# Slots of 4128 bytes instead of 4096, and 39 of them instead of 40

## The chip, the cores and the metric

The kernel runs on one core of a Trainium2 chip. Time is the device time of one execution in microseconds (us); of several runs the median is given. Beside the time of a run stands its span: from the first to the last instruction of the program that the profiler recorded.

A core has TensorE (PE in the profile, its weight loads PEld), VectorE (DVE), ScalarE (ACT), GpSimd (POOL) and SyncE (SP), each with its own queue of instructions that it takes in order. DMAs are issued from the queues of SP and POOL and move data by 16 DMA engines. The engines wait for each other by semaphores. The on-chip memory has 128 partitions; an address below is a byte within a partition.

## The reference

All in float32. With `xn` the normalised input (8192 tokens of 512 numbers),

```
out = x + attention(xn) + moe(xn)

attention: feats   = 1/sqrt(512) * exp(xis) * exp(xn @ (xis*proj).T - 0.5*|xn|^2 * xis^2)
           weights = the same of input_weights
           out     = feats @ weights.T                                   (512 x 512)

moe:       scores = sigmoid(xn @ router_w)                               (64 experts)
           4 of 8 groups of experts by their best score, of these the 8 best experts
           weights of the 8: scores / their sum * 2.5
           each expert takes its first 256 tokens:
             (silu(t @ gate_w[e]) * (t @ up_w[e])) @ down_w[e]           (512 -> 256 -> 512)
           out = weighted sum over the experts + a shared expert of the same form
```

## The kernel before

**Products.** Each float32 operand is split in two (`upper` on ScalarE writes the high part as float32r, `rest` on VectorE the low part), and `products` makes three passes of matmuls: high by high, high by low, low by high. So a weight tile that a DMA brings is first split into two further tiles, and only these are read by TensorE.

**Stages.** The token blocks of 512 (16 of them) go through `look_up` (turned by TensorE, routed, their rows written to `xnw` in HBM) and, every second one, through `dense` (shared expert and attention); this takes the first 400 us or so. Then comes the loop over the 64 experts (`for i in range(E + 1)`), with the attention of the other blocks (`late_attention`) put between its steps. At its end `ends` does the shared expert of the remaining blocks, from about 1146 us on.

**An expert.** At step `i` of the loop SyncE is given the loads of the gate and up weights of expert `i + 2` (`load_gates`, L744, two tiles) and the down weights of expert `i + 1` (`load_down`, L749, one tile). TensorE does `hidden(i)`: 48 matmuls for gate and up, and the 8 transposes of the rows of expert `i + 1` (`turn_slots`, L773), which `gather` (L756) has brought. Then ScalarE and VectorE split the gates of expert `i + 1` (`split_gates`), TensorE does `down(i - 1)` (12 matmuls), and POOL adds its rows to the output by an indirect DMA (L831). Then the down weights of expert `i` are split (`split_down`).

**The slots.** Nearly all large tiles stand in one pool, `four`, with one tag: `kib4` hands out a slot of it. A tile of 128 partitions by 1024 float32 numbers fills 4096 bytes of each partition. Which slot a tile gets and what it waits for is settled when the program is built: the first instruction that writes a tile (a DMA for loads, an engine for others) waits for the last reader of the tile that had the slot before. All slots of a pool's tag have the size of the largest tile asked for under the tag.

In the loop over the experts, an expert takes 12 slots: 2 for gate and up, 4 for their splits, 1 for down, 2 for its splits, 2 for the turned rows `gT`, 1 for `ehT`. The line search (`at`) takes one more for each four experts, and the seven blocks of `late_attention` take 10 each (4 `xT`, 4 `fU`, 2 `yb`), spread over the 64 experts. Eleven slots are held through the whole loop: `fW` 4, `pT` 4, `ye` 3.

In the built program the first slot begins at byte 25504 of a partition, and the others follow each other at once. The pools `rows` (gathered rows), `rt` (small tiles) and `act` (work tiles of 2048 bytes) follow behind the slots; `const` stands ahead of them.

Of the kernel before, what the change touches and what calls it, by code (L numbers as in the profile page):

```python
# [11 lines left out]
I32 = mybir.dt.int32  # L12
# [6 lines left out]
P = 128  # L19
# [3 lines left out]
E = 64  # L23
# [12 lines left out]
RC = R // P  # L36
IC = I // P
NH = CAP // P
SLOTS4 = 40
UT = TB // 2  # L40
GAP = 5
NCH = T // P
# [11 lines left out]
def rfs_attention_moe_kernel(  # L54
# [23 lines left out]

    four = ctx.enter_context(tc.tile_pool(name="four", bufs=SLOTS4))
    rows = ctx.enter_context(tc.tile_pool(name="rows", bufs=4))  # L80
# [3 lines left out]
    def kib4(shape, name, dt=FPR):  # L84
        return four.tile(shape, dt, tag="four", name=name)
# [131 lines left out]
    nc.gpsimd.iota(slot_i, pattern=[[P, NH]], base=0, channel_multiplier=1)  # L217
    slot = const.tile([P, NH], FP, name="slot")
    nc.gpsimd.tensor_copy(slot, slot_i)
    erow_i = kib4([P, E], "erow_i", I32)  # L220
    nc.gpsimd.iota(erow_i, pattern=[[1, E]], base=-E, channel_multiplier=0)
    erow = const.tile([P, E], FP, name="erow")
    nc.gpsimd.tensor_copy(erow, erow_i)
# [782 lines left out]
```

## Time and profile before

| | |
|---|---|
| three runs | 1308.88, 1309.06, 1309.46 us; median 1309.06 |
| the profiled execution | 1309.75 us, span 1308.0 us |
| granted TensorE clock | 0.999 |
| PE busy | 1295.1 us of the span (99%), 7648 matmuls |
| DVE, ACT, POOL busy | 925.9 (71%), 644.1 (49%), 587.0 (45%) us |
| DMA | 338.61 MB, mean 259 GB/s |

The page gives busy time by engine, the same over 40 slices of the span, the DMA queues, the chain of work that ended last, and groups of equal instructions with the mean of one, the idle time of the engine ahead of them and what ended it. Three more views of the trace are used: the waits (who waited for whom, in total, how often, the longest), the stages (busy time of each engine between two times), and the timeline (instructions in the order of time). SPq is the queue of SyncE, which issues DMAs; a wait of SPq is time in which its next DMA could not be issued yet.

### The profile page before, as it was taken

What the parts mean: (1) busy time and instruction counts of PE and PEld (TensorE: products, weight loads), DVE (VectorE), ACT (ScalarE), POOL (GpSimd) and SP (SyncE); (2) the same over time, 40 slices, a digit from 0 to 9 for tenths busy, and PEclk for the clock granted to TensorE, in tenths of its full rate; (3) what the DMA queues carried; (4) which work ended last, traced back from release to release, by engine and by line L of the source; (5) the groups of instructions that cost most, each with busy time, mean ns of one, the idle gap of its engine ahead of it and who ended that gap; (6) DMA issues with size and microseconds to landing.
All of it is one profiled execution on the core that took longest, in us unless ns stands there. A gap on an engine that the chain in (4) does not pass through costs nothing.

```text
span 1308.0 us, 21401 instructions
## 1 busy us (share of the span) xinstructions
PE 1295.1 (99%) x7648; PEld 1136.1 (87%) x7648; DVE 925.9 (71%) x1922; ACT 644.1 (49%) x1017; POOL 587.0 (45%) x692
## 2 busy tenths in 40 slices
PE   8999999999999999999999999999999999999998
PEld 6888888888888988999999999999999999988886
DVE  7978768867765776678677677777776776643555
ACT  5643544454432555566566465656665565540111
POOL 3122022123106766777677767767766654210000
PEclk9999999999999999999999999999999999999999
DMA  7655675675586989999999999999999999784995
GB/s 255 242 209 207 242 282 200 240 286 212 198 306 191 308 236 322 263 288 274 303 288 251 282 290 270 264 302 290 275 257 297 286 260 238 204 240 167 319 319 193
DMA packets 189498, 338.61 MB, mean 259 GB/s; under 512 B 15952, under 2 KB 87632, under 8 KB 189392
## 3 DMA queue, kind: packets, MB, share of 16 engines
q1 hardware_dynamic: 153456, 245.93, 54.4%
q0 software_dynamic: 35936, 91.32, 29.8%
q8 instruction: 60, 0.98, 0.3%
q14 instruction: 46, 0.38, 0.1%
HBM read 220.66 MB, written 104.99 MB: 249 GB/s over the span
## 4 chain that ended last, share of the span: by engine, by line
PE 87%; DVE 7%; DMA 3%; SPq 1%; issue 1%; ACT 1%; POOL 0%; ACTq 0%; DVEq 0%
PE ps_gu L108 41%; PE ps_e L108 13%; PE ps_o L108 12%; PE ps_fu L108 6%; PE ps_y L108 5%; PE ps_t L773 3%; PE ps_f L108 3%; PE ps_x L333 2%; PE ps_l L366 1%; DMA xb<-in_L_attn_x_dram 1%; DVE st L277 1%; DVE f L495 1%; SPq L264 1%; DVE xT_l L101 1%; DVE fT L101 1%
## 5 line engine op out<-in xcount | busy, mean ns | idle before, releaser
L831 POOL DMA_INDIRECT out_dram<-ye,who x128 | 232.7, 1818 | 181.5 <-ACT ye L830 120.8
L108 PE MATMUL ps_gu<-gT,gu_h 128*128 128x256 f32 x2048 | 292.5, 285 | 0.0
L108 PEld LDWEIGHTS ps_gu<-gT,gu_h 128*128 128x128 f32 x2048 | 265.4, 190 | 8.9 <-ACT gu_h L98 4.7
L703 POOL DMA_INDIRECT at<-upto,line x128 | 131.9, 1030 | 76.0 <-DVE first_of L697 37.3
L101 DVE TENSOR_TENSOR gu_l<-gu,gu_h 128x1024 fp32r<-128x1024 f32 x128 | 155.0, 1221 | 14.3 <-ACT gu_h L98 13.4
L108 PE MATMUL ps_gu<-gT,gu_l 128*128 128x256 f32 x1024 | 164.9, 283 | 0.0
L756 POOL DMA_INDIRECT xg<-xnw,who x128 | 141.7, 1107 | 40.0 <-issue 30.0
L108 PE MATMUL ps_e<-d_h,ehT 128*128 128x512 f32 x512 | 147.8, 390 | 0.0
L108 PEld LDWEIGHTS ps_gu<-gT,gu_l 128*128 128x128 f32 x1024 | 142.6, 191 | 3.4 <-DVE gu_l L101 0.7
L98 ACT CAST gu_h<-gu 128x1024 fp32r<-128x1024 f32 x128 | 132.1, 1047 | 0.0
L830 ACT ACTIVATE ye<-ps_e,we 128x512 f32<-128x512 f32 x128 | 87.6, 687 | 84.5 <-PE ps_e L108 84.2
L108 PEld LDWEIGHTS ps_e<-d_h,ehT 128*128 128x128 f32 x512 | 94.7, 188 | 18.8 <-ACT d_h L98 0.2
L98 ACT CAST ehT<-sg 128x512 fp32r<-128x512 f32 x64 | 39.9, 623 | 123.1 <-DVE sg L503 112.0
L248 POOL TENSOR_TENSOR a<-rstd,ve 128x4 f32<-128x4 f32 x45 | 10.2, 227 | 200.5 <-DVE rstd L244 198.0
L503 DVE SCALAR_TENSOR_TENSOR sg<-sg,ps_gu 128x512 f32<-128x512 f32 x64 | 43.9, 686 | 72.1 <-PE ps_gu L108 72.0
L101 DVE TENSOR_TENSOR gT<-ps_t,gT 128x512 fp32r<-128x512 f32 x128 | 82.0, 682 | 17.1 <-ACT gT L98 17.1
L101 DVE TENSOR_TENSOR d_l<-d,d_h 128x1024 fp32r<-128x1024 f32 x64 | 78.2, 1221 | 11.7 <-ACT d_h L98 11.6
L509 ACT ACTIVATE f<-f,ab 128x512 f32<-128x512 f32 x64 | 46.3, 723 | 73.1 <-DVE f L495 72.4
L108 PE MATMUL ps_o<-fW_h,fT 128*128 128x512 f32 x288 | 79.8, 391 | 0.2 <-ACT fT L98 0.2
L108 PE MATMUL ps_e<-d_l,ehT 128*128 128x512 f32 x256 | 79.2, 390 | 0.0
L108 PE MATMUL ps_o<-d_h,hT 128*128 128x512 f32 x256 | 79.1, 396 | 0.0
L501 ACT ACTIVATE sg<-ps_gu 128x512 f32<-128x512 f32 x64 | 38.2, 597 | 77.7 <-PE ps_gu L108 77.7
(181 smaller groups left out, 2520.0 us busy)
## 6 DMA issues: line engine op xcount, KB each, us to landing
gu<-in_L_ffn_gate_w_dram SPq DMA_DIRECT2D x64, 512.0 KB
gu<-in_L_ffn_up_w_dram SPq DMA_DIRECT2D x64, 512.0 KB
d<-in_L_ffn_down_w_dram SPq DMA_DIRECT2D x64, 512.0 KB
xnw<-xw SPq DMA_DIRECT2D x32, 577.0 KB
xb<-in_L_attn_x_dram SPq DMA_DIRECT2D x32, 512.0 KB
out_dram<-xb SPq DMA_DIRECT2D x32, 512.0 KB
xT_h<-turned SPq DMA_DIRECT2D x30, 512.0 KB
xT_l<-turned SPq DMA_DIRECT2D x30, 512.0 KB
```

Of the source, the lines that this page charges most:

```text
L98: return nc.scalar.copy(dst, src)
L101: return on.tensor_tensor(dst, src, hi.bitcast(FP), ALU.subtract)
L108: last["pe"] = nc.tensor.matmul(ps, w[c][a], v[c][b], start=(start and part == 0 and c == 0), stop=(stop and part == 2 and c == n - 1),)
L333: last["turn"] = nc.tensor.transpose(pr[:, ts(s, P)], src(s)[:, ts(kc, P)], ident if dt is FP else ident_r)
L501: nc.scalar.activation(dst, g, AF.Tanh, scale=0.5)
L503: nc.vector.scalar_tensor_tensor(dst, dst, 0.5, u, ALU.mult, ALU.mult)
L509: nc.scalar.activation(f, f, AF.Exp, scale=ab[:, rc : rc + 1])
L703: nc.gpsimd.indirect_dma_start(out=at[:, e % TE, h, :], out_offset=None, in_=upto, in_offset=bass.IndirectOffsetOnAxis(ap=line[:, e, h : h ...
L756: nc.gpsimd.indirect_dma_start(out=xgs[e][:, h, :], out_offset=None, in_=xnw, in_offset=bass.IndirectOffsetOnAxis(ap=who[:, e, h : h + 1], ...
L773: turned_s = nc.tensor.transpose(pr[:, c, ts(h, P)], xr[:, h, ts(c2 * 2 + c, P)], ident_r)
L830: nc.scalar.activation(ye[:, h, :], po, AF.Copy, scale=wes[e][:, h : h + 1])
L831: now = nc.gpsimd.indirect_dma_start(out=out, out_offset=bass.IndirectOffsetOnAxis(ap=who[:, e, h : h + 1], axis=0), in_=ye[:, h, :], in_o ...
```

## The change

```diff
-SLOTS4 = 40
+SLOTS4 = 39
...
-    erow_i = kib4([P, E], "erow_i", I32)
+    erow_i = kib4([P, 1032], "erow_i", I32)[:, 0:E]
```

`erow_i` is a small tile of the beginning, used once. Asked for with 1032 numbers it makes 4128 bytes the size of every slot of the pool; of it, the same 64 columns are used as before. 40 slots of 4096 bytes are 163,840 bytes of a partition; 39 slots of 4128 are 160,992. Every tile that filled a slot leaves the last 32 bytes of it unused.

In the built program every engine has the same instructions in the same order. What differs: the slot that a tile stands in, and so its address and what its first writer waits for; the slots begin at 25504, 29632, 33760, ... instead of 25504, 29600, 33696, ...; and `rows`, `rt` and `act` begin 2848 bytes lower.

## The prediction

> **What bounds the kernel now.** I read first the busy time by engine, then the stages, then the waits of TensorE, and last the waits of SyncE's queue, because the change touches a kernel's supply of tiles.
>
> ```profile
> PE 1295.1 (99%) x7648; PEld 1136.1 (87%) x7648; DVE 925.9 (71%) x1922; ACT 644.1 (49%) x1017; POOL 587.0 (45%) x692
> ...
> PE   8999999999999999999999999999999999999998
> DMA  7655675675586989999999999999999999784995
> ```
>
> TensorE has work for 1295.1 of 1308.0 us; the other engines have a quarter of their time or more to spare. DMA is at nine tenths from about 430 us on, so loads deserve a look. Busy PE is a model, so the waits must say the same. Those of PE and PEld:
>
> ```profile
> PE ps_x L333 <- DMA wi<-_attn_input_weights_dram: 4.8, 2, 3.6
> PE ps_bu L447 <- DVE prior_r L437: 1.0, 4, 0.3
> ...
> PEld ps_gu L108 <- ACT gu_h L98: 4.9, 16, 0.4
> PEld ps_x L333 <- POOL padded L256: 3.5, 1, 3.5
> ```
>
> The numbers are the total, the count and the longest. Apart from the start (`wi` must land) nothing holds TensorE for more than fractions of a microsecond. The stage 600 to 700 us, all inside the loop over the experts, as columns PE, PEld, DVE, ACT, POOL, granted clock, DMA share, GB/s:
>
> ```profile
> 600.00:700.00 100.00, 100.00 (x683) 92.20 (x682) 74.48 (x114) 58.34 (x84) 71.28 (x55) 1.00 1.00 287
> ```
>
> TensorE sets the time there, at full clock. Now the queue that the slots do hold back, in the window of the expert loop (430 to 1140 us):
>
> ```profile
> SPq L744 <- PE ps_gu L108: 191.8, 37, 10.0
> SPq L744 <- DVE gu_l L101: 88.5, 24, 6.6
> ...
> SPq L744 <- PE ps_e L108: 59.5, 23, 8.1
> ```
>
> L744 issues the gate and up loads. SyncE stands 340 us in these three rows alone, waiting for the last reader of the tile that had the slot before. So the slots do limit how early a load starts; whether that matters depends on when the load is needed.
>
> **The change part by part.**
>
> *One slot fewer.* An expert takes 12 slots; `at` adds 16/64 = 0.25 and `late_attention` 7 × 10/64 = 1.1, together 13.3. An expert lasts as long as TensorE takes for it: 68 matmuls and transposes of its own and 7 × 96/64 = 10.5 of the late attention, 78.5, at 683 in 100 us: 11.5 us. So a slot is handed out every 11.5/13.3 = 0.86 us. Eleven slots are held through the loop; of the other 29 one goes. A tile is then given a slot that is freed one hand-out later: on average 0.86 us later. Slots are freed in bursts, so single loads move by nothing or by several us; the longest single wait of SPq above, 10.0 us, is the upper bound that I take, nothing the lower. The value is 0.86 us, since it follows from counts.
>
> Against this stands how early the loads are. The timeline of SPq and ACT around 805 to 845 us:
>
> ```profile
> 805.21 1.50 SPq L744 DMA_DIRECT2D gu<-in_L_ffn_up_w_dram  x1
> 806.82 0.45 SPq L749 DMA_DIRECT2D d<-in_L_ffn_down_w_dram  x1
> ```
>
> ```profile
> 827.65 2.00 ACT L98 CAST gu_h<-gu 128x1024 fp32r<-128x1024 f32 x2
> ...
> 835.75 1.05 ACT L98 CAST d_h<-d 128x1024 fp32r<-128x1024 f32 x1
> ```
>
> The tile issued at 805.21 is split as the second of the two at 827.65, some 23 us later; the down tile issued at 806.82 is split at 835.75, 29 us later (another down tile, issued an expert before, stands between them). The landing of a load is the last update of its semaphore. Over the 128 gate and up loads it comes 7.7 us (median; longest 15.9) after the issue, and the split follows at least 8.4 us later (median 16); over the 64 down loads 10.2 us (longest 18.1), at least 7.1 us left. So a mean delay of 0.86 us is taken from a reserve of at least 7.1 us: **0 us**. The cover is that reserve; if it is gone, ScalarE waits at the split for the load, and behind it the `gT` of the next expert and the scaling of `ye`, which TensorE and POOL wait for. That ACT does not wait for such loads now can be seen in its group, whose idle time has no DMA as its end:
>
> ```profile
> L98 ACT CAST gu_h<-gu 128x1024 fp32r<-128x1024 f32 x128 | 132.1, 1047 | 0.0
> ```
>
> A rule of the Trainium skill speaks against the change here: its page Perfetto Trace Analysis, section Optimization Strategy, says that a gap repeating on the engine that should be saturated can mean too little room for the next tile, by the number of buffers. If TensorE had such gaps and each expert gained one hand-out, the sum would be 64 × 0.86 = 55 us, 1364 us. The rows show no such gap (PE 100.00 of 100.00), so I count 0.
>
> Other tiles that take slots: `xT` of the last stage is the tightest. Its low half is used 1.0 to 3 us after landing (from 1209 us on). But SPq there stands in L163 for the result that it stores (91.7 us in total for `xo`), not in L576 for a slot, so its loads do not move. The `xb` loads of the first stage have nothing in reserve in places (the chain has 1% of the span, 13 us, in their DMA); SPq waits for slots at L151 by 1.5 us in four cases, so I allow 0 to 4 × 0.86 = 3.4 us there and take 0: in that stage slots are freed by work long past. Engines that write a slot themselves (`gT`, `ehT`, `fU`, the splits) get one freed some 28 hand-outs before, 24 us; 0.
>
> *Addresses.* The DMAs first. No row before tells apart two starts, since all slots of the program before begin at 160 past a multiple of 256 (25504 and steps of 4096). The skill's page DMA: Bandwidth & Descriptors, section How a descriptor splits into AXI transactions, says that a transaction begins at a multiple of 256 bytes and that the bytes ahead of an unaligned start cost beats of 32 bytes. By it each piece now costs 5 beats too many; with steps of 4128 the starts spread over all eight multiples of 32, a mean of 3.5. A gate piece of 1024 bytes goes from 37 to 35.5 beats (-4%), a piece of 2048 bytes from 69 to 67.5 (-2%). If landing followed beats, a gate load would land 0.3 us earlier (an estimate: 4% of 7.7), which nothing waits for; the 13 us of `xb` in the chain would shrink by 2%, 0.3 us. By the rows, where loads mostly wait for each other, it is 0. I take 0 and keep -0.3; and +0.3 the other way, since the rule is not shown here for writes.
>
> The engines. Operations of one shape cost the same in and out of the slots:
>
> ```profile
> L101 DVE TENSOR_TENSOR gT<-ps_t,gT 128x512 fp32r<-128x512 f32 x128 | 82.0, 682 | 17.1 <-ACT gT L98 17.1
> L101 DVE TENSOR_TENSOR ehT<-sg,ehT 128x512 fp32r<-128x512 f32 x64 | 44.0, 688 | 26.1 <-ACT ehT L98 26.1
> ...
> L108 PEld LDWEIGHTS ps_f<-xT_h,pT_l 128*128 128x128 f32 x144 | 27.0, 188 | 5.6
> L366 PEld LDWEIGHTS ps_l<-xT_l,rwp 128*128 128x128 f32 x64 | 12.0, 188 | 2.7
> ```
>
> `sg` stands in `act`, `rwp` in `const`, not 4096 bytes apart from anything. If distances of a multiple of 4096 cost something, the slots' rows would be longer. 0 us.
>
> *Sum.* Span 1308.0 + 0 (slots) + 0 (addresses) = 1308.0; the profiled execution took 1309.75, that is 1.75 around the span, and was 0.7 above the median of the runs, 1309.06. Predicted: **1309.0 us**, the median unchanged.
>
> **The rivals.**
>
> *Slower by loads that come late.* The mechanism is the first edit with the upper bound: bursts make a freed slot late by up to 10 us instead of 0.86. It decides from about 7 us on, the smallest reserve. At 10 us, four places in the loop run short (loads issued around 429, 795, 865 and 877 us, with reserves of 8.8, 7.1, 8.4 and 8.4 us), by 1.2 + 2.9 + 1.6 + 1.6 = 7.3 us: 1316 us. For it: SPq's long waits. Against it: the mean is an eighth of the bound.
>
> *Engines that read or write at another speed.* One nanosecond on each of 7648 matmuls is 7.6 us, so 1301 or 1317 us. For it: TensorE is the bound, and nothing hides it. Against it: the equal rows above, which cover the weight loads, not the moving operand.
>
> *Faster by DMAs.* The -0.3 us above, at most some 2 us if all `xb` loads gain a tenth: 1307 to 1308.7, within 0.2%.
>
> *That nothing changes because the size is not taken up* is excluded: the built program has the slots 4128 bytes apart.
>
> **How the numbers follow.** 0.2% is 2.6 us, about what a measurement of this kernel can tell from no change. All hidden (with the DMA gain in it): 0.80. Late loads: 0.10, slower. Engines slower 0.04, engines faster 0.06. So faster 0.06, same 0.80, slower 0.14. The likeliest case reaches from 1307 (DMA gain) to 1311 (half of the 3.4 us at `xb`); the range takes that and the smaller late loads (one place of 2.9 us added to 1309.5): 1307.0 to 1312.5.
>
> **What would show it.** Right: PE and PEld waits as before; in the loop, as in the trace before, 227 ns from the start of a matmul of 512 columns to the next (median) and 120 of 256; SPq's waits at L744 some tens of us longer; no wait of ACT `gu_h` or `d_h` for a DMA. Wrong by slots: rows `ACT gu_h L98 <- DMA gu` or `ACT d_h L98 <- DMA d`, with PE idle after them. Wrong by addresses: another mean for the same shape of a matmul, cast or subtraction, or other times to landing.

## The result

| | before | after |
|---|---|---|
| median of four runs | 1309.26 us (1308.88 to 1310.26) | 1315.80 us (1315.13 to 1316.76) |
| span of the profiled execution | 1308.0 us | 1314.3 us |

The ratio is 1.005, 95% interval 1.0037 to 1.0062: the change makes the kernel slower by half a per cent, outside the predicted range of 1307.0 to 1312.5 us.

The page of the kernel after, busy time by engine and the slices of PE and DMA:

```profile
PE 1301.7 (99%) x7648; PEld 1131.3 (86%) x7648; DVE 927.0 (71%) x1922; ACT 644.0 (49%) x1017; POOL 586.5 (45%) x692
...
PE   8999999999999999999999999999999999999998
...
DMA  7655675675586989999999999999999999784995
```

TensorE has the same 7648 matmuls and 6.6 us more to do; the other engines differ from before by 1.1 us at most. Did it wait? The waits of PE and PEld after:

```profile
PE ps_x L333 <- DMA wi<-_attn_input_weights_dram: 6.0, 3, 3.6
PE ps_lt L383 <- ACT lt L376: 0.8, 2, 0.7
```

```profile
PEld ps_gu L108 <- ACT gu_h L98: 3.6, 12, 0.4
PEld ps_x L333 <- POOL padded L256: 3.6, 1, 3.6
```

No new wait of more than 1 us, and less waiting for `gu_h` than before (4.9 us). Nor does ScalarE wait for the load of an expert's weights; its group of casts still has no idle time ahead of it:

```profile
L98 ACT CAST gu_h<-gu 128x1024 fp32r<-128x1024 f32 x128 | 132.0, 1046 | 0.0
```

So the time is in the matmuls themselves. The chain of work in the order of time, from 1160 us on, where TensorE does little but matmuls of 512 columns; columns are start, length, what, how many matmuls. Before:

```profile
1160.13 10.88 PE ps_f L108 x48
1171.01 5.44 PE ps_gu L108 x24
1176.45 12.24 PE ps_o L108 x54
1188.69 5.44 PE ps_gu L108 x24
```

After:

```profile
1163.61 11.16 PE ps_f L108 x48
1174.77 5.57 PE ps_gu L108 x24
1180.34 12.54 PE ps_o L108 x54
1192.88 5.57 PE ps_gu L108 x24
```

24 matmuls took 5.44 us and now take 5.57: 227 and 232 ns each, and so within 0.03 us in every group of 24 of this stage. In the loop over the experts the groups of 24 matmuls of 256 columns behind those of 512 went the other way. Before (the same view, at 717 us):

```profile
717.40 2.87 PE ps_gu L108 x24
```

After (at 609 us):

```profile
609.44 2.83 PE ps_gu L108 x24
```

Over the whole trace I took the time from the start of each matmul to the start of the next, between matmuls of one width, without the first interval of each stretch of such matmuls and without the longer gaps (over 253 ns for 512 columns, over 147 ns for 256). This mean is called the pace below. It went from 227.7 to 232.1 ns for 512 columns and from 119.7 to 118.1 ns for 256.

That is the whole difference. Added up over pairs of equal matmuls in the two traces: 3547 intervals that begin with a matmul of 512 columns give +14.6 us, 2999 with one of 256 columns -4.5 us, longer gaps became 3.1 us shorter (2.1 us of it in the first 410 us, as if stalls that are waited for anyway took up some of the slower pace), and the rest gives -0.7: +6.3 us, as the spans say (1314.3 - 1308.0). By stage it is +3.5 us up to 414 us, -0.5 in the loop over the experts, where both widths meet, and +3.3 from 1139 us on.

### The profile page after: what moved, and what is told of

Read it like the earlier page. It is cut to its first block, busy times and chain, and to the rows that moved or that the text cites. A ratio compares the mean times of both kernels' runs of the same rounds, so it can differ in the third digit from the quotient of the medians.

```text
span 1314.3 us, 21375 instructions
## 1 busy us (share of the span) xinstructions
PE 1301.7 (99%) x7648; PEld 1131.3 (86%) x7648; DVE 927.0 (71%) x1922; ACT 644.0 (49%) x1017; POOL 586.5 (45%) x692
## 4 chain that ended last, share of the span: by engine, by line
PE 96%; DVE 2%; ACT 0%; DMA 0%; issue 0%; POOL 0%; SPq 0%; DVEq 0%; ACTq 0%
PE ps_gu L108 41%; PE ps_o L108 14%; PE ps_e L108 14%; PE ps_f L108 8%; PE ps_y L108 6%; PE ps_fu L108 6%; PE ps_t L773 3%; PE ps_l L366 2%; PE ps_x L333 2%; PE ps_lt L383 1%; PE ps_bu L458 0%; DMA wi<-_attn_input_weights_dram 0%; DVE st L277 0%; DVE xo L549 0%; DVE pT_l L101 0%
## 5 line engine op out<-in xcount | busy, mean ns | idle before, releaser
L108 PE MATMUL ps_gu<-gT,gu_h 128*128 128x256 f32 x2048 | 289.3, 283 | 0.0
L756 POOL DMA_INDIRECT xg<-xnw,who x128 | 138.3, 1080 | 40.1 <-issue 29.6
```

The lines of the kernel that those rows point to most:

```text
L108: last["pe"] = nc.tensor.matmul(ps, w[c][a], v[c][b], start=(start and part == 0 and c == 0), stop=(stop and part == 2 and c == n - 1),)
L756: nc.gpsimd.indirect_dma_start(out=xgs[e][:, h, :], out_offset=None, in_=xnw, in_offset=bass.IndirectOffsetOnAxis(ap=who[:, e, h : h + 1], ...
```

## The experiments

The first theory after the result: what changed for TensorE is only where its operands stand. Slots of 4096 bytes put moving operand and weights at a *distance* (start of the moving operand less start of the weights) that is a multiple of 4096 plus multiples of 512 inside the tiles; slots of 4128 give distances of 0, 32, ... 224 past a multiple of 256. Theory A: the pace depends on that distance. Theory B: the missing slot. Theory C: the start of an operand by itself.

The next four kernels ran on one chip, on which the kernel before took 1331.57 us (median, at a granted clock of 0.990 to 0.997 instead of 0.999); every ratio below is to the kernel before on the same chip.

**Count alone.**

```diff
-SLOTS4 = 40
+SLOTS4 = 39
```

> Only the count: 39 slots of 4096 bytes. Theory A (the pace of TensorE's matmuls depends on how far apart, within 256 bytes, the moving operand and the weights start; all distances here are multiples of 4096 plus offsets inside the tiles that are multiples of 512): 1309 us as before, 227 ns from start to start of matmuls of 512 columns and 120 ns of 256 columns. Theory B (the missing slot delays loads): 1316 us as with the whole change.

Measured: 1330.39 us, ratio 0.9986 (0.9971 to 1.0001); pace 227.7 and 119.6 ns. Theory B falls.

**Distance alone.**

```diff
-    erow_i = kib4([P, E], "erow_i", I32)
+    erow_i = kib4([P, 1032], "erow_i", I32)[:, 0:E]
```

> Only the distance: 40 slots of 4128 bytes. Theory A: 1316 us (1315 to 1317), 232 ns for 512 columns and 118 ns for 256 columns as with the whole change. Theory B: 1309 us.

Measured: 1338.37 us, ratio 1.0057 (1.0039 to 1.0074), 6.8 us more; pace 232.1 and 118.0 ns. The whole effect is in this line. (`rows`, `rt` and `act` move by 1280 bytes here, a multiple of 256, so their place within 256 bytes is not the cause.)

**Start of all slots, 32 bytes on.**

```diff
+    const.tile([P, 8], FP, name="spare")
     four = ctx.enter_context(tc.tile_pool(name="four", bufs=SLOTS4))
```

> 40 slots of 4096 bytes, but the first begins 32 bytes later, at 192 past a multiple of 256 instead of 160. Theory A (only the distance between two operands counts): 1309 us, 227 and 120 ns. Theory C (the start of an operand itself counts, by its place within 64 or 256 bytes; after the change half of the starts are multiples of 64, none was before, and here all are): 1316 us or farther from 1309, with another pace of the matmuls.

Measured: 1332.21 us, ratio 1.0009 (0.9996 to 1.0022); pace 227.7 and 119.6 ns. In the built program all slots now begin at multiples of 64. Theory C falls for this shift; with it agrees that in the trace after, the pace of 512 columns is 231.8 to 232.4 ns for every one of the eight starts of the moving operand within 256 bytes (by the addresses of the built program), and 231.6 to 232.3 for those of the weights.

**38 slots, 4352 bytes apart.**

```diff
-SLOTS4 = 40
+SLOTS4 = 38
-    erow_i = kib4([P, E], "erow_i", I32)
+    erow_i = kib4([P, 1088], "erow_i", I32)[:, 0:E]
```

> 38 slots of 4352 bytes (17 times 256), so that distances are multiples of 256 and seldom of 4096. Theory A with a period of 256 bytes: 1309 us, 227 and 120 ns. Theory A with a longer period (512 to 4096 bytes): 1313 us or more, pace as with 4128. Theory B: slower than 1316 us, since two slots are missing.

Measured: 1331.20 us, ratio 0.9992 (0.9977 to 1.0007); pace 227.7 and 119.6 ns. A distance need only be a multiple of 256, and two slots fewer cost nothing that can be measured either. The same pieces of the chain with 40 slots of 4128 bytes:

```profile
1184.60 11.17 PE ps_f L108 x48
1195.77 5.58 PE ps_gu L108 x24
1201.34 12.55 PE ps_o L108 x54
```

and with 38 of 4352:

```profile
1181.79 10.88 PE ps_f L108 x48
1192.67 5.44 PE ps_gu L108 x24
1198.11 12.24 PE ps_o L108 x54
```

**39 slots, 4224 bytes apart**, another chip (before: 1328.73 us):

```diff
-SLOTS4 = 40
+SLOTS4 = 39
-    erow_i = kib4([P, E], "erow_i", I32)
+    erow_i = kib4([P, 1056], "erow_i", I32)[:, 0:E]
```

> 39 slots of 4224 bytes (4096 + 128): distances are 0 or 128 past a multiple of 256. Theory A with a period of 256 bytes: between the two, 512 columns at 229 to 232 ns, 256 columns at 118 to 120 ns, a ratio to the kernel before of 1.002 to 1.005. A period of 128 bytes would give the pace and the time of before (ratio 1.000).

Measured: 1337.66 us, ratio 1.0059 (1.0039 to 1.0079); pace 231.2 and 118.9 ns. So 128 bytes is not a period. The paces lie where expected; the ratio is above the upper end that I gave, since I had counted on half of the matmuls keeping 227 ns, and only few did. Why is seen under "What runs before".

**The matmuls alone.** The body of the kernel is replaced by this (cut at `...`), so nothing of the model is computed; `weights` and `moving` are two tiles in float32r. It was run once.

```
for cols in (512, 256):
    for order in (range(8), range(7, -1, -1)):
        for shift in order:
            ps = ps_mm.tile([P, cols], FP, tag="mm", name=f"by_{words[shift]}")
            for n in range(64):
                at = n % 4 * P + shift * 8
                nc.tensor.matmul(ps, weights[:, ts(n % 8, P)], moving[:, at : at + cols], ...)
```

> Matmuls alone, nothing of the model: one weight tile and one moving tile, 64 matmuls for each of eight distances between them (0, 32, ... 224 bytes past a multiple of 256), for 512 and for 256 columns, once with growing and once with falling distance; no other engine works meanwhile, and all outputs but the last are thrown away, the last stands for the whole output. Theory A: from start to start at distance 0: 227 ns for 512 columns and 120 ns for 256 columns; at the other distances 230 to 234 ns for 512 columns, and for 256 columns 113 to 118 ns at 192 and no uniform value at the others. Theory D (the pace comes from what other engines or DMAs do at the same addresses): the same pace at all eight distances.

The timeline of PE, `by_six` being a distance of 192 and `by_two` of 64; columns are start, length of 64 matmuls, what. First 512, then 256 columns:

```profile
21.80 15.10 PE L93 MATMUL by_one<-moving,weights 128*128 128x512 f32 x64
36.73 14.82 PE L93 MATMUL by_two<-moving,weights 128*128 128x512 f32 x64
...
260.08 7.70 PE L93 MATMUL by_two<-moving,weights 128*128 128x256 f32 x64
...
312.81 7.45 PE L93 MATMUL by_six<-moving,weights 128*128 128x256 f32 x64
...
357.87 7.83 PE L93 MATMUL by_none<-moving,weights 128*128 128x256 f32 x64
```

From start to start, without the first eight of each 64, mean of both directions (512 columns at 0: the falling one alone, since the first ten intervals of this program were 418 to 594 ns). Below it the kernel after, with the distance that each matmul has by the addresses of the built program:

| distance past a multiple of 256 | 0 | 32 | 64 | 96 | 128 | 160 | 192 | 224 | mean |
|---|---|---|---|---|---|---|---|---|---|
| 512 columns alone, ns | 226.7 | 233.3 | 228.9 | 233.3 | 232.8 | 234.3 | 233.3 | 233.3 | 232.0 |
| 256 columns alone, ns | 120.0 | 117.2 | 117.8 | 120.0 | 118.7 | 117.3 | 113.3 | 118.3 | 117.8 |
| 512 columns in the kernel after, ns | 231.2 | 231.6 | 231.7 | 233.1 | 231.7 | 232.5 | 232.0 | 232.4 | 232.1 |
| 256 columns in the kernel after, ns | 118.6 | 117.7 | 117.5 | 119.0 | 118.4 | 118.2 | 117.3 | 118.3 | 118.1 |

For the matmuls alone the left column is near the kernel before (227.7 and 119.7), and the mean over all eight near the kernel after (232.1 and 118.1). But that second agreement is in part luck: distance by distance the kernel after does not follow the table. Its 512-column matmuls took 231 to 233 ns at every distance, at 0 too. "What runs before" has the reason. Between 50 and 365 us, when the last matmuls began, no other engine computed, the DMA engines' share was 0.00 and the granted clock 1.00, so theory D (others at the same addresses) falls. So does the start of the moving operand by itself: 160 past a multiple of 256 it is the start of all 512-column matmuls of the kernel before (227.7 ns), and here the one at distance 32 (233.3 ns). For 512 columns 0 is the best distance there is at this step; for 256 columns 192 is, and 0 and 96 are the worst.

**gT at 192.** The table says that the 3072 matmuls of 256 columns in `hidden` could be faster than in either kernel, if `gT` alone stood elsewhere. The control first (36 slots for the rest, four for `gT`, at distance 0):

```diff
-SLOTS4 = 40
+SLOTS4 = 36
+    gts = ctx.enter_context(tc.tile_pool(name="gts", bufs=4))
     rows = ctx.enter_context(tc.tile_pool(name="rows", bufs=4))
...
-        gp = [kib4([P, KC, CAP], "gT") for _ in range(2)]
+        gp = [gts.tile([P, KC, CAP], FPR, tag="gts", name="gT") for _ in range(2)]
```

> 36 slots of 4096 bytes, and four more of the same size in a pool of their own for gT alone (the moving operand of the experts' 256-column matmuls), at distance 0 (multiples of 256 bytes) from the weights. It is the control for the next kernel: by theory A the pace stays at 227 and 120 ns, ratio to the kernel before 1.000; slower by some tenths of a per cent if 36 slots are too few for the rest.

and then with a filler of 192 bytes ahead of `gts` and one of 64 behind it:

```diff
+    pad = ctx.enter_context(tc.tile_pool(name="pad", bufs=1))
+    pad.tile([P, 48], FP, name="pad0")
     gts = ctx.enter_context(tc.tile_pool(name="gts", bufs=4))
+    pad1 = ctx.enter_context(tc.tile_pool(name="pad1", bufs=1))
+    pad1.tile([P, 16], FP, name="pad1")
```

> The same, but the pool of gT begins 192 bytes later (and a filler behind it), so that in the experts' 256-column matmuls the moving operand starts 192 bytes past a multiple of 256 from the weights; all 512-column matmuls keep distance 0. Theory A, from the matmuls run alone: 113.3 instead of 120.0 ns for 3072 matmuls, 20 us less; ratio to the kernel before 0.985 (0.983 to 0.990), 512 columns unchanged at 227 ns. If the pace inside the kernel is set by something else: 1.000.

Measured on one chip (before: 1308.97 us): the control 1306.82 us, ratio 0.9984 (0.9977 to 0.9991), pace 227.7 and 119.7 ns; with 192 bytes 1297.30 us, ratio 0.9912 (0.9895 to 0.9929), pace 227.5 and 116.4 ns. It is faster than both kernels, by 9.5 us against the control, half of the 20 us expected. Control and kernel have the same order of instructions, and of the 9.7 us between their spans 3004 intervals of 256 columns give 9.3. The control itself is 2.1 us faster than the kernel before, which I had not expected; TensorE has its matmuls in another order there, and whether that is the cause is not shown. The trace shows which half is missing. The chain of the kernel with 192 bytes:

```profile
708.00 2.72 PE ps_e L113 x12
710.72 2.83 PE ps_gu L113 x24
713.55 0.62 PE ps_t L778 x8
714.18 2.81 PE ps_gu L113 x24
```

The 24 behind the 512-column `ps_e` take 2.83 us, 118 ns each. The 24 behind the transposes take 2.81 us with a first interval of 188 ns and four of 114 to 121; from there on each takes 113 to 114 ns, to the end. Within a group nothing differs in the distance, which is 192 throughout. Over the whole trace, without the first six intervals of each group, the median is 117.8 ns in the 64 groups behind 512 columns and 113.4 in the 63 behind transposes.

**What runs before.** That asks whether a distance has more than one pace. Alone again, and run once; `group(name, columns, shift in numbers of 4 bytes, count)` writes `count` matmuls:

```
for first, count in ((512, 12), (128, 8)):
    for step in range(32):
        group("entry", first, 0, count)                    # distance 0
        group(f"from_...", 256, 2 * step, 24)              # distance 8 * step bytes
```

> Matmuls alone again (nothing of the model is computed). In the kernel with gT at 192 the 256-column matmuls ran at 113 ns after transposes and at 118 ns after 512-column matmuls. Here each of 32 distances (0 to 248 bytes in steps of 8) has 24 matmuls of 256 columns behind 12 of 512 columns at distance 0, and then the same behind 8 of 128 columns. Theory A1 (two stable paces at one distance, and what ran before chooses): at 192, 117 to 118 ns behind 512 columns and 113 to 114 ns behind 128 columns. Theory A2 (the difference in the kernel comes from other things, such as the accesses of the other engines): 113 to 114 ns behind both. If some distance has 113 to 114 ns behind both, gT placed there should bring the kernel to about 20 us under its control.

At 192, from start to start in ns, behind 512 columns and behind 128:

```
117 118 118 117 118 118 118 117 119 117 118 118 117 118 118 118 117 119 117 118 118 117 118
170 120 117 116 114 113 114 113 113 114 113 113 114 113 113 114 113 113 114 113 113 114 113
```

Theory A1 holds: two stable paces at one distance, and what ran before chooses. Within 24 matmuls it did not change over. It is not only 192: at 16, 72, 80, 144 and 160 bytes, too, the last twelve of the 24 differed by 1.7 to 1.8 ns between the two, at 72 and 144 with the group behind 512 columns as the faster one.

The same memory is behind the kernel after. At distance 0 a matmul of 512 columns reaches 227 ns only after some others at that distance: alone, behind those at 32, the intervals were 230, 236, 228, 232, 231 and then 227. By the addresses of the built program, the first seven intervals of a stretch of matmuls at distance 0 have a mean of 230.6 ns in the kernel before and the later ones, 2523 of them, 226.9. In the kernel after, 1359 of the 1647 stretches of 512-column matmuls with one distance are two matmuls long and 602 of the 704 of 256 columns four long. Of its 294 intervals at distance 0 only four come later than the seventh of their stretch; these took 226.5 ns, the others 231.3. With 4224 bytes it is 231.1 for the first seven and 227.9 for the 168 later ones. So what costs time in the kernel after is, as far as these numbers go, above all that the distance changes all the time.

One distance of the 32 reached 113.4 ns behind both: 112 bytes, after about ten matmuls (mean of the 23 intervals behind 512 columns 115.0, and behind 128 columns, without the first, 115.5; with the first it is 117.9, which the expectation of the next run leaves out). At 104 bytes both ran at 130 ns, the slowest.

**gT at 112.** Tiles of `gts` of 1088 numbers, used from number 28 on (against the control):

```diff
-        gp = [gts.tile([P, KC, CAP], FPR, tag="gts", name="gT") for _ in range(2)]
+        gp = [gts.tile([P, 1088], FPR, tag="gts", name="gT")[:, 28 : 28 + KC * CAP]
+              .rearrange("p (c n) -> p c n", c=KC) for _ in range(2)]
```

> As with gT in a pool of its own, but its tiles begin 112 bytes past a multiple of 256 from the weights (28 numbers into slots of 4352 bytes). Alone, 24 matmuls of 256 columns at this distance took a mean of 115.1 ns behind 512 columns as well as behind 128 columns; at 192 it was 117.8 and 113.5. Theory A1: a mean of 115 to 116 ns in the kernel, ratio to the kernel before 0.988 to 0.992, about as with 192. If the pace in the kernel does not follow the matmuls alone at this distance: 118 ns or more, ratio 0.994 or more.

Measured on another chip (before: 1328.37 us): 1311.39 us, ratio 0.9867 (0.9847 to 0.9887), pace 227.7 and 115.6 ns. The pace is as expected, the ratio a little better: 17.0 us less than before, where 4.1 ns on 3072 matmuls would be 12.6. (The 20 us that the expectation under "What runs before" held out for such a distance are not reached: some ten of the 24 matmuls pass before the pace is 113 ns.) The rest of the 17.0 us is not explained; there was no control at distance 0 on this chip, and the order of TensorE's matmuls is again another one. In its chain the group behind the 512-column matmuls is now the shorter one:

```profile
703.52 2.72 PE ps_e L109 x12
706.24 2.76 PE ps_gu L109 x24
709.00 0.64 PE ps_t L779 x8
709.64 2.85 PE ps_gu L109 x24
```

Both versions once more, side by side on one chip (before: 1326.89 us):

> gT at 112 and gT at 192 on one chip, since the two were timed on different chips before. From the pace in the two traces (115.6 and 116.4 ns for 256 columns, 3072 of them) 112 should be 2.7 us or 0.2% faster than 192: ratio to the kernel before 0.989 with 192 at 0.991. If the chip made the difference of the earlier runs (0.987 against 0.991), the two come out within 0.3% of each other.

> As above: ratio to the kernel before 0.991, and 0.2% above the kernel with 112.

Measured: 1315.98 us, ratio 0.9910 (0.9884 to 0.9937), with 112, and 1317.96 us, ratio 0.9935 (0.9918 to 0.9951), with 192. The medians are 2.0 us apart, near the 2.7 expected, but the intervals overlap, and the two kernels differ in the order of TensorE's matmuls too. So both beat the kernel before, by 0.6 to 1.3% of the time in two measurements each; that 112 is the better is not shown.

## Why the prediction was wrong

*What bounds the kernel.* Right: TensorE, without waits. It is the reason why 4 ns on a matmul appear in the time at all.

*One slot fewer, 0 us.* Right, shown by the count alone (0.9986) and by 38 slots (0.9992). The waits of SyncE after, in the loop over the experts:

```profile
SPq L744 <- PE ps_gu L108: 121.6, 27, 9.5
SPq L744 <- PE ps_e L108: 110.1, 31, 10.4
...
SPq L744 <- DVE d_l L101: 60.9, 12, 7.1
SPq L744 <- DVE gu_l L101: 48.2, 13, 10.8
```

The queue waits for other releasers, but the reserve held: the split of a weight tile follows its landing by at least 7.7 us (7.1 before). The waits at L744 did not grow by some tens of us, as the prediction had it: all its rows in the loop come to 394 us after and 395 before. That such waiting delayed nothing on TensorE, and that one slot less cost nothing, is the part of the working that can be reused.

*Addresses, DMAs, 0 us with -0.3 to +0.3.* In the time nothing of it can be seen, as expected. The mean from issue to landing of the gate and up loads was 8.0 us before and 7.7 after, but on the chip where count and distance were changed one at a time it was 7.5 us with 4096 bytes and 7.7 with 4128. The prediction's estimate of 4%, from the rule of the Trainium skill (DMA: Bandwidth & Descriptors, section How a descriptor splits into AXI transactions) that bytes ahead of a start that is no multiple of 256 cost beats, is not seen in these means.

*Addresses, the engines, 0 us.* This is the step that failed: "Operations of one shape cost the same in and out of the slots" and "If distances of a multiple of 4096 cost something, the slots' rows would be longer." It stood at 0 us; alone, the new distances cost 6.8 us (ratio 1.0057). Two things were wrong with it. I compared rows of VectorE, and of TensorE only weight loads; those of `ps_f` have a length of 188 ns in both kernels, whatever the pace. And I asked only whether a distance of 0 costs something, so a loss from leaving it was no case. The trace before had the answer in small: `ps_l` takes its weights from `rwp`, 64 bytes away from the distance of all others, and 64 of its intervals (without the first three of each group of eight) have a mean of 229.2 ns, beside 226.9 for the settled ones at distance 0; the matmuls alone gave 228.9 at 64. That `rwp` stands elsewhere was even an argument of the prediction. The lengths that the page gives for matmuls are modelled, but between the two kernels they moved as the pace did. Before:

```profile
L108 PE MATMUL ps_gu<-gT,gu_h 128*128 128x256 f32 x2048 | 292.5, 285 | 0.0
L108 PE MATMUL ps_o<-fW_h,fT 128*128 128x512 f32 x288 | 79.8, 391 | 0.2 <-ACT fT L98 0.2
```

After:

```profile
L108 PE MATMUL ps_gu<-gT,gu_h 128*128 128x256 f32 x2048 | 289.3, 283 | 0.0
L108 PE MATMUL ps_o<-fW_h,fT 128*128 128x512 f32 x288 | 81.1, 395 | 0.0
```

*The rivals.* "Engines that read or write at another speed" is what happened, at 1317 us by my estimate of 1 ns on each matmul, with a chance of 0.04 for slower. That 1317 is near 1315.8 is luck: the 1 ns stood for +4.4 ns on the wide and -1.6 on the narrow matmuls, which nearly cancel in the loop over the experts (-0.5 us). "Late loads" did not happen: no ACT row waits for `gu` or `d`. The last paragraph of the prediction named the sign to look for, another time from matmul to matmul, and that is the one that came.

## What to carry to other kernels

When a change moves addresses, what a bound TensorE does with them is a term of the sum like any other: read the time from one matmul's start to the next, not the length of a weight load. Where moving operand and weights stand in equal slots, keep the slots' size a multiple of 256 bytes, or measure the distances in question with a kernel that does nothing but those matmuls; eight distances and two widths fit into one run. Where the distance stays the same over a long stretch of matmuls, as in the kernel before and with `gT` at 112, its pace was within 1 ns of that of the matmuls alone. Where the distance changes every two to four matmuls, as in the kernel after, only the mean agreed; there the order of what runs would have to be copied too. The number of slots and their size are two changes, and here only the size counted.

## What the runs showed that I had not expected

- The pace of float32r matmuls with a weight load for each depends on the distance between moving operand and weights modulo 256 bytes: 226.7 to 234.3 ns for 512 columns and 113.3 to 120.0 ns for 256 at steps of 32 bytes, up to 130 ns at 104 bytes. That the period is 256 bytes is shown by slots of 4352 and 4224 bytes in the kernel.
- The best distance for one width is not the best for the other: 0 for 512 columns, and for 256 columns 192 or 112, with 0 among the slow ones. No kernel was run with all its 512-column matmuls at another distance.
- At a distance of 192 there are two stable paces, 117.8 and 113.4 ns, and what ran before decides between them. At a distance of 0 a matmul of 512 columns needs some seven others at 0 before it to run at 227 instead of 231 ns.
- That the two streams of reads of TensorE meet in some unit that repeats every 256 bytes would fit this; it is an inference from the paces. Which unit it is, and why the pace has a memory, stays open: no run here looked at more than starts of matmuls.
